# A second layer's attention weighed one sequence later, its chances transposed by VectorE and two trips through memory

## The chip, the cores and the metric

The kernel runs on one core of a Trainium2 chip. A core has five engines that work side by side, each with its own instruction queue: TensorE for matrix products (PE in the profile; PEld is its loading of weights), VectorE (DVE), ScalarE (ACT), GpSimd (POOL) and SyncE (SP), which here issues DMAs. Engines wait for each other by semaphores. The metric is the device time of one execution in microseconds (us), as the median of several runs.

## The reference, cut to what matters

The input is x, 8 sequences of 512 tokens with 256 channels, in f32. Two layers follow each other. The first (16 heads of attention with rotary embedding, plus a product with 8-bit weights) is not touched. The second, for each sequence b, is:

```python
xn = layernorm(x)
left, right = xn @ compare_left, xn @ compare_right            # 512 x 64 each
comparison = left @ right.T / sqrt(256)                        # 512 x 512
mask  = comparison > threshold
gated = softmax(comparison + gate_bias)
attn  = (mask * gated) @ xn
prev  = xn shifted by one token
xr, xk = mu_r * xn + (1 - mu_r) * prev, mu_k * xn + (1 - mu_k) * prev
ffn   = sigmoid(xr @ W_r.T) * (relu(xk @ W_k.T) ** 2 @ W_v.T)
out   = x + attn + ffn
```

`mask * gated` before its division by the row sums is called the chances below. The product `chances @ xn` needs the chances with keys in the partitions, while the comparison leaves them with queries in the partitions, so they are transposed in between.

## The kernel before

All of it is one program, written out instruction by instruction for each engine; nothing reorders it later. Each engine executes its instructions in the order in which the Python text issues them, so the order of the calls in the loop over sequences (`for b in range(B)`, L1002) is the order of work on every engine. Tiles come from pools whose buffers go round; a tile waits until the last reader of the buffer's former tile is done. PSUM has eight banks, handed out in turn by `bank`.

A sequence of layer 2 is made of these steps:

- `norm` (L223): mean and variance of x1 on DVE, the power -1/2 on POOL, and, in the function that it returns, four normalising operations on DVE.
- `turn_input` (L228): eight transposes on PE (`pyt`) and two copies by ACT give xn with channels in the partitions (`yt`).
- `sides_of` (L240): left and right by PE (`plr`), a copy by ACT, and two DMAs on SP's queue (L249, L250) that exchange the upper and lower halves of `lr`.
- `mix_before` and `mix_own` (L653, L662): the two mixtures with the token before, s = 1 for the key and s = 0 for the gate. ACT writes (1 - mu) times the token before, DVE adds mu times the token.
- `compare` (L670): four products `c`, their row maxima on DVE (L685, L689), the exponential with its row sums on ACT (L694), and on DVE the mask times the exponential (L697, tile `e`).
- `key`, `gate`, `value` (L703, L717, L731): the feed-forward part, products `pk`, `pg` and `pvv` on PE, the squares of kk and the sum with x1 on POOL, the product with the gate on DVE.
- `turn_chances` (L743): sixteen transposes on PE (`trc`, L749), and four copies out of PSUM, two by ACT and two by DVE, into `ptc`.
- `end` (L756): the weighing. 16 products `po` in two halves, whose weights are the transposed chances, the division by the row sums and the sum with the rest on DVE (L768), and the store of `y`.
- `clip_late`, `complete`, `round_late`, `fetch_late` (L644, L649, L641, L634): the last piece of layer 1 for sequences two and three ahead: a clip on DVE to bf16 (`xq`, L197 and L201), products `acc` on PE, `u` on DVE (L215), a sum on POOL (L218), and their loads.

In the loop, iteration b does compare and key of b, then the input, mixtures and sides of b + 1 in between the gate and value of b, then the transposes of b's chances, complete, and last the weighing of b itself, with the norm of b + 2 between its halves. Layer 1 uses a similar transposition for its own input: `turn_x` (L320) turns squares of 32 x 32 on DVE (L325) and moves them through memory.

Of the kernel before, what the change touches and what calls it, by code (L numbers as in the profile page):

```python
# [16 lines left out]
P = 128  # L17
B, S, D = 8, 512, 256
H, L = 16, 64
NT = S // P  # L20
# [24 lines left out]
def two_layers(  # L45
# [214 lines left out]
    with ExitStack() as c0:  # L260
# [151 lines left out]
        def finish(at):  # L412
            for half in range(2):
                output_product(at, half)
                add_output(at, half)
# [218 lines left out]
        def fetch_late(b):  # L634
            if b < B - 1:
                tag, k = {2: ("vr", 0), 3: ("vr", 1), 4: ("t1", 0), 5: ("t1", 1), 6: ("t2", 0)}[b]
                fetch_output(b, by_tokens(cuts[tag][k]))
            if b > 2:
                late[b] = fetch_input(b, cuts["wo"][b % 2])
# [4 lines left out]
        def clip_late(b):  # L644
            xq = work.tile([P, NK * S], BF16, tag="xq", name=f"xq_{b}")
            clip(late.pop(b), xq)
            return xq

        def complete(b, xq):  # L649
            for half in range(2):  # L650
                add_quantised(b, half, xq, line(f"u_{b}_{half}"))

        def mix_before(b, s):  # L653
            mx = work.tile([P, NK, S], F32, tag="yl"[s], name=f"mix_{b}_{s}", bufs=2)
            for k in range(NK):
                nc.scalar.activation(
                    mx[:, k, :], xts[b][:, k, :S], AF.Copy,
                    scale=nmus[:, s * NK + k : s * NK + k + 1],
                )
            mixed[b, s] = mx  # L660

        def mix_own(b, s):  # L662
            mx = mixed[b, s]
            for k in range(NK):
                nc.vector.scalar_tensor_tensor(
                    mx[:, k, :], xts[b][:, k, 1:], gs[:, s * NK + k : s * NK + k + 1], mx[:, k, :],
                    ALU.mult, ALU.add,
                )

        def compare(b):  # L670
            one, two = lr.pop(b)
            es = [qk.tile([P, 2, S], F32, tag="h0", name=f"e_{b}_{n}") for n in range(2)]
            nm = small.tile([P, NT], F32, tag="nm4", name=f"nm4_{b}", bufs=2)
            nb = small.tile([P, NT], F32, tag="nb4", name=f"nb4_{b}", bufs=2)
            sm = small.tile([P, NT], F32, tag="sm4", name=f"sm4_{b}", bufs=2)
            rs = small.tile([P, NT], F32, tag="rs4", name=f"rs4_{b}", bufs=2)
            cs_ = [bank(f"c_{b}_{i}") for i in range(NT)]
            for i in range(NT):
                left, right = (one, two) if i % 2 == 0 else (two, one)
                rows = slice(i % 2 * KC, i % 2 * KC + KC)  # L680
                nc.tensor.matmul(  # L681
                    cs_[i], left[rows, bass.ts(i, P)], right[rows, :], start=True, stop=True
                )
            for i, c in enumerate(cs_):
                nc.vector.tensor_reduce(nm[:, i : i + 1], c, AX.X, ALU.max, negate=True)  # L685
                if i % 2:

                    two_ = slice(i - 1, i + 1)
                    nc.vector.tensor_scalar(  # L689
                        nb[:, two_], nm[:, two_], tg[:, 1:2], tg[:, 1:2], ALU.subtract, ALU.add  # L690
                    )
            for i, c in enumerate(cs_):
                e = es[i // 2][:, i % 2, :]
                nc.scalar.activation(  # L694
                    e, c, AF.Exp, bias=nb[:, i : i + 1], accum_out=sm[:, i : i + 1]
                )
                nc.vector.scalar_tensor_tensor(  # L697
                    e, c, tg[:, 0:1], e, ALU.is_gt, ALU.mult
                )
            nc.vector.reciprocal(rs, sm)  # L700
            pcs[b], sums[b] = es, rs

        def key(b):  # L703
            xk = mixed.pop((b, 1))
            kk = prob.tile([P, NK, S], F32, tag="p", name=f"kk_{b}")
            for m in range(NK):
                pb = bank(f"pk_{b}_{m}")
                for k in range(NK):
                    nc.tensor.matmul(  # L709
                        pb, w2[:, 1, k, bass.ts(m, P)], xk[:, k, :],  # L710
                        start=(k == 0), stop=(k == NK - 1),
                    )
                nc.scalar.activation(kk[:, m, :], pb, AF.Relu)
                nc.gpsimd.tensor_tensor(kk[:, m, :], kk[:, m, :], kk[:, m, :], ALU.mult)
            return kk
# [15 lines left out]
        def value(b, half, r, kk):  # L731
# [8 lines left out]
            nc.vector.tensor_tensor(r[:, rows, :], pb, r[:, rows, :], ALU.mult)  # L740
            nc.gpsimd.tensor_tensor(r[:, rows, :], r[:, rows, :], x1s[b][:, rows, :], ALU.add)

        def turn_chances(b):  # L743
            es = pcs.pop(b)
            pt = [qk.tile([P, 2, NT, P], F32, tag="h1", name=f"ptc_{b}_{n}") for n in range(2)]
            for i in range(NT):
                tr = bank(f"trc_{b}_{i}").rearrange("p (m n) -> p m n", m=NT)
                for m in range(NT):
                    nc.tensor.transpose(tr[:, m, :], es[i // 2][:, i % 2, bass.ts(m, P)], ident)  # L749
                if i % 2 == 0:  # L750
                    nc.scalar.copy(pt[i // 2][:, i % 2], tr)
                else:
                    nc.vector.tensor_copy(pt[i // 2][:, i % 2], tr)
            return pt

        def end(b, ats, pt, r, y):  # L756
            rs, xn = sums[b], xns[b]
            for at in ats:
                po = bank(f"po_{b}_{at}").rearrange("p (j n) -> p j n", j=2)
                for j in range(2):  # L760
                    for m in range(NT):
                        nc.tensor.matmul(  # L762
                            po[:, j, :], pt[at // 2][:, j, m, :], xn[:, m, :],
                            start=(m == 0), stop=(m == NT - 1),
                        )
                for j in range(2):
                    i = at + j
                    nc.vector.scalar_tensor_tensor(  # L768
                        y[:, i, :], po[:, j, :], rs[:, i : i + 1], r[:, i, :],
                        ALU.mult, ALU.add,  # L770
                    )

                    if b == B - 1:
                        nc.sync.dma_start(out[b].rearrange("(t p) c -> p t c", p=P)[:, i, :], y[:, i, :])
                if b < B - 1:
                    nc.sync.dma_start(
                        out[b].rearrange("(t p) c -> p t c", p=P)[:, at : at + 2, :], y[:, at : at + 2, :]
                    )
# [220 lines left out]
            value(0, half, r, kk)  # L999
        compare(0)  # L1000
        finish(at)
        for b in range(B):  # L1002
            if b == 0:
                cut(prob, [P, 2, 4 * pitch(1) + 1, Q], "t1", 2)
                cut(prob, [P, 2, 4 * pitch(2) + 1, Q], "t2", 1)
                cut(work, [P, NP, D], "wo", 2)
            if b + 3 < B:
                fetch_late(b + 3)
            if b > 0:
                compare(b)  # L1010
                kk = key(b)
            if b + 1 < B:
                turn_input(b + 1, whole(f"yt_{b + 1}", S + 1))
            if b > 0 and b + 2 < B:
                xq = clip_late(b + 2)
            if b + 1 < B:
                mix_before(b + 1, 1)
                mix_own(b + 1, 1)
            if b == 0:
                pt = turn_chances(b)  # L1020
            else:
                r = gate(b)
            if b + 1 < B:
                sides_of(
                    b + 1, *(attp.tile([P, S], F32, tag="att", name=f"lr_{b + 1}_{n}") for n in range(2))
                )
            if b + 1 < B:
                mix_before(b + 1, 0)
            if b > 0:
                for half in range(2):  # L1030
                    value(b, half, r, kk)
            if b + 3 < B:
                round_late(b + 3)
            if b > 0:
                pt = turn_chances(b)
            if b + 2 < B:
                complete(b + 2, xq)
            if b + 1 < B:
                mix_own(b + 1, 0)
            y = work.tile([P, NT, D], F32, tag="v", name=f"y_{b}", bufs=2)  # L1040
            end(b, (0,), pt, r, y)
            if b + 2 < B:
                normal = norm(b + 2, by_tokens(cuts["t0"][(b + 2) % 3]))
            end(b, (2,), pt, r, y)
            if b + 2 < B:
                normal()


def _layouts(i):
# [63 lines left out]
```

## Time and profile before

| | before |
|---|---|
| median of 3 runs | 938.59 us (937.72 to 939.12) |
| the profiled execution | 939.52 us, span 937.7 us |
| granted TensorE clock | 0.996 |
| PE busy | 920.2 us, 98% |
| DVE busy | 794.8 us, 85% |
| ACT busy | 527.4 us, 56% |
| POOL busy | 543.3 us, 58% |
| one sequence of layer 2, 839.75 to 864.40 | 24.65 us: PE 24.65, DVE 21.00, ACT 12.59, POOL 10.09 busy |

The page's span counts from the first to the last instruction; the run's own time is 1.8 us longer. An engine's busy time says how much of the span it works, not whether it is waited for: that is read from the chain of waits, which follows each instruction back to what released it. Rows by tile give the shortest, median and longest duration in ns and the number of instructions. f32 products appear as two records each, so 16 products of `po` are 32 records.

### The profile page before, as it was taken

The page shows a single profiled execution, that of the slowest core. Times are in us where ns is not written, and L with a number is a line of the kernel's source. Part 1 is how long each engine was busy: PE and PEld are TensorE (multiplying, and loading weights), DVE is VectorE, ACT ScalarE, POOL GpSimd, SP SyncE. Part 2 cuts the span into 40 slices and gives each one's busy share as a digit, 9 for nine tenths or more (in the row PEclk, how much of TensorE's full clock was granted, in tenths as well). Part 3 has the DMA queues.
Part 4 walks back from the last instruction along what each step waited for, and adds up shares of the span by engine and source line. Part 5 has one row for each costly group of instructions (what it writes and reads, how often), then busy time and mean ns, then how long its engine had stood idle before and what let it go on. Part 6 is the DMA issues. An engine that isn't in the chain of part 4 may idle for free.

```text
span 937.7 us, 27410 instructions
## 1 busy us (share of the span) xinstructions
PE 920.2 (98%) x10443; PEld 595.8 (64%) x10443; DVE 794.8 (85%) x2443; ACT 527.4 (56%) x1476; POOL 543.3 (58%) x688
## 2 busy tenths in 40 slices
PE   8999998999999999999999999999999999999998
PEld 5446565666565666657575656566657777777776
DVE  4997789897989889988998899899899588888854
ACT  3575555555564656564657465556667434445553
POOL 2576667566665566476756756688666424444311
PEclk9999999999999999999999999999999999999999
DMA  6757454435552554346534645554444132221011
GB/s 205 200 154 195 110 128 148 111 88 135 171 121 77 134 168 112 101 99 182 136 74 120 177 108 123 172 143 107 101 116 126 48 101 75 71 59 45 23 34 34
DMA packets 68706, 108.55 MB, mean 116 GB/s; under 512 B 8416, under 2 KB 47328, under 8 KB 68576
## 3 DMA queue, kind: packets, MB, share of 16 engines
q1 hardware_dynamic: 66704, 105.16, 42.1%
q10 hardware_dynamic: 1872, 1.64, 0.7%
q8 instruction: 83, 1.36, 0.6%
q14 instruction: 47, 0.39, 0.1%
HBM read 42.29 MB, written 28.84 MB: 76 GB/s over the span
## 4 chain that ended last, share of the span: by engine, by line
PE 84%; DVE 7%; DMA 3%; issue 2%; POOL 2%; ACT 1%; SPq 1%; DVEq 0%; POOLq 0%; ACTq 0%
PE pq L434 20%; PE av L603 14%; PE sc L515 11%; PE pw L396 10%; PE pv L478 8%; PE po L762 6%; PE pk L709 3%; PE pg L724 3%; PE pvv L736 3%; DVE t L586 2%; DVE p L543 2%; PE c L681 2%; PE trc L749 1%; PE plr L245 1%; DMA y<-l 1%
## 5 line engine op out<-in xcount | busy, mean ns | idle before, releaser
L547 ACT ACTIVATE p<-p,nm 128x64 f32<-128x64 f32 (+15 forms) x512 | 260.0, 512 | 131.4 <-DVE nm L543 106.7
L566 POOL TENSOR_SCALAR p<-p,rs 128x512 f32<-128x512 f32 (+4 forms) x504 | 266.4, 552 | 44.6 <-DVE rs L558 42.5
L467 POOL TENSOR_TENSOR h<-h,y 128x1024 f32<-128x1024 f32 x62 | 161.2, 2599 | 184.3 <-DVE y L452 100.7
L543 DVE CUSTOM_DVE_ANT_0 p<-sc,cmask 128x64 f32<-128x64 f32 (+15 forms) x512 | 190.1, 434 | 52.2 <-PE sc L515 52.2
L586 DVE STREAM_TRANSPOSE t<-p 128x256 f32<-128x256 f32 (+3 forms) x640 | 192.1, 365 | 18.2 <-POOL p L566 18.2
L515 PE MATMUL sc<-h,h 64*32 64x512 f32 (+15 forms) x4096 | 137.7, 393 | 1.2 <-POOL h L467 1.2
L603 PE MATMUL av<-t,vr 32*64 32x256 f32 (+15 forms) x4096 | 130.3, 396 | 5.5 <-issue 5.5
L603 PEld LDWEIGHTS av<-t,vr 32*64 32x64 f32 x4096 | 124.3, 132 | 10.9 <-issue 9.6
L515 PEld LDWEIGHTS sc<-h,h 64*32 64x32 f32 x4096 | 78.2, 106 | 78.3 <-issue 57.7
L440 ACT ACTIVATE l<-pq,cs 128x512 f32<-128x512 f32 x128 | 84.6, 684 | 65.4 <-PE pq L434 54.3
L434 PE MATMUL pq<-xnT,wk 128*128 128x512 f32 x256 | 114.8, 601 | 3.6 <-DMA xnT<-xnf 2.4
L452 DVE TENSOR_TENSOR y<-y,cs 128x1024 f32<-128x1024 f32 x64 | 110.9, 1733 | 7.3 <-DMA y<-l 7.3
L396 PE MATMUL pw<-wo,att 128*128 128x256 f32 x512 | 114.9, 382 | 0.5 <-DVE nm L543 0.5
L434 PE MATMUL pq<-xnT,wq 128*128 128x512 f32 x256 | 114.6, 599 | 0.9 <-ACT xnT L352 0.9
L478 PE MATMUL pv<-wv,xnT 128*128 128x512 f32 x256 | 114.3, 599 | 0.0
L396 PEld LDWEIGHTS pw<-wo,att 128*128 128x128 f32 x512 | 95.9, 190 | 19.2 <-issue 6.1
L547 ACT ACTIVATION_READ_ACCUMULATOR p<-p,nm 128x1 f32 x512 | 97.5, 190 | 0.0
L434 PEld LDWEIGHTS pq<-xnT,wk 128*128 128x128 f32 x256 | 48.9, 192 | 61.5 <-issue 57.9
L452 DVE TENSOR_TENSOR h<-l,cs 128x1024 f32<-128x1024 f32 x64 | 80.0, 1251 | 4.9 <-ACT l L440 4.9
L478 PEld LDWEIGHTS pv<-wv,xnT 128*128 128x128 f32 x256 | 47.3, 190 | 57.9 <-issue 54.5
L434 PEld LDWEIGHTS pq<-xnT,wq 128*128 128x128 f32 x256 | 47.2, 190 | 56.6 <-issue 48.8
L617 ACT ACTIVATE att<-av,cs 128x512 f32<-128x512 f32 x64 | 38.8, 689 | 72.4 <-PE av L603 72.4
(114 smaller groups left out, 939.0 us busy)
## 6 DMA issues: line engine op xcount, KB each, us to landing
y<-l SPq DMA_DIRECT2D x256, 128.0 KB, 2.3
va<-v SPq DMA_DIRECT2D x32, 512.0 KB, 6.3
vr<-va SPq DMA_DIRECT2D x64, 256.0 KB, 5.0
x<-in_x SPq DMA_DIRECT2D x15, 512.0 KB, 4.2
x1f<-x SPq DMA_DIRECT2D x7, 512.0 KB, 4.3
out<-y SPq DMA_DIRECT2D x14, 256.0 KB, 2.2
xnf<-xs SPq DMA_DIRECT2D x6, 512.0 KB, 3.3
xnT<-xnf SPq DMA_DIRECT2D x24, 128.0 KB, 2.9
```

Source lines behind the costliest of these rows:

```text
L396: nc.tensor.matmul(pw[:, j, :], atts[at, p][:, tok], wo[:, 4 * (at % NH) + p, :], start=(p == 0), stop=(p == 3),)
L434: nc.tensor.matmul(pb.rearrange("p (t a r) -> p t a r", a=4, r=Q), w[:, g, k, bass.ts(t, P)], xnT[b][:, k].rearrange("p a (t r) -> p t a r ...
L440: nc.scalar.activation(l[:, t, :], pb, AF.Identity, bias=cs[:, bias : bias + 1])
L452: nc.vector.tensor_tensor(dst, src, table[:, None, :].to_broadcast([P, 2, S]), ALU.mult)
L467: (engine or nc.gpsimd).tensor_tensor(h, h, y, ALU.add)
L478: nc.tensor.matmul(pb.rearrange("p (g n) -> p g n", g=2), xnT[b][:, k, 2 * half + j], wqkv[2][:, 2 * g : 2 * g + 2, k, :], start=(k == 0), ...
L515: nc.tensor.matmul(scored[at, i][e][j * Q : j * Q + Q, :], q[rows, j % 2, bass.ts(i, Q)], k[rows, j % 2, :n], start=True, stop=True,)
L543: nc.vector.tensor_tensor_reduce(p[:, e, col : col + n], sc, cmask[:, S - n :], -1.0 / L**0.5, BIG, ALU.add, ALU.min, nm[:, c : c + 1],)
L547: nc.scalar.activation(p[:, e, col : col + n], p[:, e, col : col + n], AF.Exp, bias=nm[:, c : c + 1], scale=-1.0, accum_out=sm[:, c : c + 1],)
L566: nc.gpsimd.tensor_scalar(p, p, rs[:, c : c + 1], 1.0, ALU.mult, ALU.mult)
L586: nc.vector.transpose(turned[at][c][:, :, at_ : at_ + (n - 1) * pitch(c) + 1 : pitch(c), :], p[:, :, c * P : c * P + n * Q].rearrange("p e ...
L603: nc.tensor.matmul(banks[j][e * L : e * L + L, i * Q :], vs[at][rows, c, m, bass.ts(e, L)], t[c][rows, e, m * pitch(c) + m : m * pitch(c) ...
```

## The change

Four things change, all in layer 2.

1. For b = 1 to 6 the chances are no longer transposed on PE. In `compare`, after each pair of e operations, DVE transposes the 32 x 32 squares of the pair (two operations of 128 x 512), with the four column blocks written interleaved, so that the words of one block lie four words apart. Four DMAs on SP's queue store each of the two tiles to memory in pieces of 512 bytes. Later, four DMAs a tile load them back as rows of 4 KB, each square in its transposed place (`move`). `po` then takes its weights at every fourth word. b = 0 and b = 7 keep `turn_chances`.
2. The weighing of b = 1 to 6 (`end`) is done in iteration b + 1, after its comparison and key. The loads of b's own squares are issued behind it, and the norm of b + 1, which used to come with the weighing of b - 1, keeps its place between the halves of that weighing.
3. The order of the rest of an iteration: gate, `turn_input`, complete, `sides_of`, mixture 1, value, mixture 0. Before, mixture 1 of b + 1 stood ahead of the gate, and complete behind the value.
4. For b > 1, `mix_own` of s = 0 is done by ACT (a scaled copy into `own`) and POOL (a sum) in place of DVE.

```diff
         def mix_own(b, s):
             mx = mixed[b, s]
             for k in range(NK):
+                if b > 1 and s == 0:
+                    own = line(f"own_{b}_{k}")
+                    nc.scalar.activation(
+                        own, xts[b][:, k, 1:], AF.Copy, scale=gs[:, s * NK + k : s * NK + k + 1]
+                    )
+                    nc.gpsimd.tensor_tensor(mx[:, k, :], mx[:, k, :], own, ALU.add)
+                    continue
                 nc.vector.scalar_tensor_tensor(
...
+                if i % 2 and by_squares(b):
+                    moves.append(turn_squares(b, i // 2, es[i // 2]))
             nc.vector.reciprocal(rs, sm)
-            pcs[b], sums[b] = es, rs
+            pcs[b], sums[b] = moves or es, rs
...
+        def by_squares(b):
+            return 0 < b < B - 1
+
+        def turn_squares(b, n, e):
+            there = qk.tile([P, 4, 2, Q, NT], F32, tag="h1", name=f"stc_{b}_{n}")
+            for i in range(2):
+                nc.vector.transpose(
+                    there[:, :, i].rearrange("p m q c -> p c m q"),
+                    e[:, i, :].rearrange("p (c m k) -> p c m k", c=NT, m=4),
+                )
+            between = away.tile([Q, 4, 2, 4, Q * NT], F32, tag="sq", name=f"sq_{b}_{n}")
+            for a in range(4):
+                nc.sync.dma_start(
+                    between[:, :, :, a].rearrange("k m i x -> k (m i) x"),
+                    there[bass.ts(a, Q)].rearrange("k m i q c -> k (m i) (q c)"),
+                )
+            def move():
+                here = qk.tile([P, 2, 4, Q * NT], F32, tag="h1", name=f"ptc_{b}_{n}")
+                for m in range(4):
+                    nc.sync.dma_start(
+                        here[bass.ts(m, Q)].rearrange("k i a x -> k (i a x)"),
+                        between[:, m].rearrange("k i a x -> k (i a x)"),
+                    )
+                return here.rearrange("p i a (q c) -> p i c (a q)", c=NT)
+            return move
...
+        held = {}
         for b in range(B):
...
             if b > 0:
                 compare(b)
                 kk = key(b)
+            if b > 1:
+                end(b - 1, (0,), *held[b - 1])
+                if b + 1 < B:
+                    normal = norm(b + 1, by_tokens(cuts["t0"][(b + 1) % 3]))
+                end(b - 1, (2,), *held.pop(b - 1))
+            if by_squares(b):
+                pt = [move() for move in pcs.pop(b)]
+            if b > 1 and b + 1 < B:
+                normal()
+            if b > 0 and b + 2 < B:
+                xq = clip_late(b + 2)
+            if b > 0:
+                r = gate(b)
             if b + 1 < B:
                 turn_input(b + 1, whole(f"yt_{b + 1}", S + 1))
...
-            if b > 0:
+            if b == 0 or b == B - 1:
                 pt = turn_chances(b)
             if b + 2 < B:
                 complete(b + 2, xq)
             if b + 1 < B:
+                sides_of(
+                    b + 1, *(attp.tile([P, S], F32, tag="att", name=f"lr_{b + 1}_{n}") for n in range(2))
+                )
+                mix_before(b + 1, 1)
+                mix_own(b + 1, 1)
+            if b > 0:
+                for half in range(2):
+                    value(b, half, r, kk)
+            if b + 1 < B:
+                mix_before(b + 1, 0)
+            if b + 3 < B:
+                round_late(b + 3)
+            if b + 1 < B:
                 mix_own(b + 1, 0)
+            if by_squares(b):
+                held[b] = pt, r, y
+            else:
+                end(b, (0,), pt, r, y)
+                if b == 0:
+                    normal = norm(b + 2, by_tokens(cuts["t0"][(b + 2) % 3]))
+                end(b, (2,), pt, r, y)
+                if b == 0:
+                    normal()
```

More of the change, by code (lines that the diff above doesn't have):

```diff
@@ L691, in compare @@
                     )
+            moves = []
             for i, c in enumerate(cs_):
@@ L762, in end @@
                         nc.tensor.matmul(
-                            po[:, j, :], pt[at // 2][:, j, m, :], xn[:, m, :],
+                            po[:, j, :], pt[at // 2][:, j, m], xn[:, m, :],
                             start=(m == 0), stop=(m == NT - 1),
@@ L1008, in two_layers @@
                 fetch_late(b + 3)
+            y = work.tile([P, NT, D], F32, tag="v", name=f"y_{b}", bufs=2)
             if b > 0:
@@ L1011, in two_layers @@
                 kk = key(b)
+            if b > 1:
[11 more added lines that the diff above has]
+                r = gate(b)
             if b + 1 < B:
                 turn_input(b + 1, whole(f"yt_{b + 1}", S + 1))
[L1014 to L1019, printed above, removed]
+            if b == 0 or b == B - 1:
                 pt = turn_chances(b)
-            else:
-                r = gate(b)
+            if b + 2 < B:
+                complete(b + 2, xq)
             if b + 1 < B:
@@ L1026, in two_layers @@
                 )
-            if b + 1 < B:
-                mix_before(b + 1, 0)
+                mix_before(b + 1, 1)
+                mix_own(b + 1, 1)
             if b > 0:
@@ L1031, in two_layers @@
                     value(b, half, r, kk)
+            if b + 1 < B:
+                mix_before(b + 1, 0)
             if b + 3 < B:
                 round_late(b + 3)
-            if b > 0:
-                pt = turn_chances(b)
-            if b + 2 < B:
-                complete(b + 2, xq)
             if b + 1 < B:
                 mix_own(b + 1, 0)
[L1040 to L1046, printed above, removed]
+            if by_squares(b):
[7 more added lines that the diff above has]
+                    normal()
 def _layouts(i):
```

## The prediction

> **What bounds the kernel now.** I read the page's first part, then the chain of waits through layer 2, then the busy time of one sequence, then the rows of what the change touches. The edit lies wholly in layer 2's loop, from 765 us on, so its price is read there. The page's busy times, and one sequence of the loop (the row's columns: length, then busy time with instructions of PE, PEld, DVE, ACT and POOL, granted clock, DMA share, GB/s):
>
> ```profile
> PE 920.2 (98%) x10443; PEld 595.8 (64%) x10443; DVE 794.8 (85%) x2443; ACT 527.4 (56%) x1476; POOL 543.3 (58%) x688
> ...
> 839.75:864.40 24.65, 24.65 (x119) 18.39 (x118) 21.00 (x43) 12.59 (x23) 10.09 (x8) 1.00 0.19 54
> ```
>
> PE is never idle in those 24.65 us, at full clock, and DVE has 21.0 us of work. The chain in order of time over the same sequence (start, length, work):
>
> ```profile
> 839.75 1.92 PE c L681 x8
> 841.67 3.63 PE pk L709 x8
> 845.30 0.87 PE pyt L234 x8
> 846.18 3.52 PE pg L724 x16
> 849.70 1.72 PE plr L245 x4
> 851.41 3.45 PE pvv L736 x16
> 854.87 1.75 PE trc L749 x16
> 856.61 0.87 PE acc L209 x8
> 857.49 6.91 PE po L762 x32
> ```
>
> Only PE stands there: what leaves PE shortens the layer, as long as nothing makes PE wait. The rows that price the change (ns min/median/max, first and last start):
>
> ```profile
> L749 PEld LDWEIGHTS trc<-ident,e x128: 139/141/142, 754.4 to 926.6; 128*128 128x128 f32 x128
> L762 PEld LDWEIGHTS po<-cut_t,ptc x224: 190/190/192, 783.4 to 933.3; 128*128 128x128 f32 x112
> L325 DVE STREAM_TRANSPOSE xs<-x x12: 668/676/702, 151.4 to 599.6; 128x512 f32<-128x512 f32 x12
> L201 DVE TENSOR_SCALAR xq<-xq x8: 426/1144/1147, 598.5 to 873.6; 128x1024 bf16<-128x1024 bf16 x8
> L665 DVE SCALAR_TENSOR_TENSOR mix<-yt,gs,mix x32: 736/752/1754, 707.8 to 907.2; 128x512 f32<-128x512 f32 x32
> L249 SPq DMA_DIRECT2D lr<-lr x7: 467/467/468, 758.8 to 902.1; - x7
> ```
>
> Of the DMA issues, with KB and median us to landing:
>
> ```profile
> cut_wo<-xnf SPq DMA_DIRECT2D x12, 128.0 KB, 4.8
> ```
>
> L325 is the same transpose of squares in layer 1, with runs of 32 written together. L201 takes 0.43 us alone and 1.14 beside a POOL operation, L665 0.74 alone and up to 1.75.
>
> **Step 1, PE's transposes go.** Six sequences lose trc: 6 x 1.75 = -10.5 us, all on the path. ACT loses two copies of 0.59 each time, DVE two of 0.69.
>
> **Step 2, DVE's load.** Per squared sequence DVE gains four transposes. By L325 one is 0.676, and 0.6 where the next one overlaps it by 0.08, as e's four of 0.74 do in 2.72: +2.4 us. It loses the two copies (1.4) and, from b + 1 = 2 on, the two mix_0 operations, which beside POOL's L218 took 2.9 us together. So DVE has about 19 of 21 us left, PE 24.65 - 1.75 = 22.9. No row writes every fourth word as these do; bounds: 0.676 (nothing makes it faster than runs) and twice that, 1.35. I take 0.676, as it is the same operation, size and type.
>
> **Step 3, the new order, walked through one steady sequence** (us from the first c). PE: c to 1.92, pk to 5.55, po of the sequence before to 12.46, pg to 15.96, pyt to 16.83, acc to 17.70, plr to 19.42, pvv to 22.87. DVE: free of the last gate product at 0.9; four maxima with nb take 3.03 in the row (842.15 to 845.18), to 3.9; four e of 2.72 together and four transposes, to 9.1; first y to 10.0 (its po ended at 9.0); norm statistics 1.9, to 11.9; POOL's power 1.2, to 13.1; four normalisations 1.3, to 14.4; clip. In the old order clip took 2.14 because POOL squared kk beside it; now POOL is done at about 8.3, so the alone price holds (0.64 + 0.43): 15.5. PE needs the normalised input at 15.96 (1.5 to spare) and xq at 16.83 (1.3 to spare). This is the tightest place on DVE. The new waits before it queue the maxima, e, transposes, y, norm and clip on DVE; who waits behind them is pyt and acc on PE.
> ACT: sigmoid, yt copies, then lr's copy at 19.42 to 20.05; mix_before to 21.4, mix_own on DVE to 22.2, gate products to 23.7, where the next DVE period began. complete now stands ahead: its u takes DVE to 19.0 and POOL's two sums from 18.2 to 20.8, before mix_own's 20.8; if they meet, mix_own takes 2.9 (the row beside L218) for 1.4, and the 1.3 of slack is just used up. round_late (1.12 on POOL) goes ahead of the new adds. ACT's four extra passes for mix_0 (two of them new, 0.75 each) end near 1.2 of the next sequence, before nb at 2.3, with the 1.28 table load ending at 2.4: cover 0, cost if it goes 0.2. POOL's two adds (1.27 each by L218's lowest) end near 6.3 and pg reads them at 12.5; kk follows at 8.3 and pvv reads it at 19.4. Both are covered.
>
> **Step 4, DMAs.** Each squared sequence adds 16 issues of 128 KB on SP's queue: 8 stores in 512-byte pieces, 8 loads in 4 KB rows; the two out stores move between them. An issue is 0.3 to 0.6 us in the rows, 0.43 typical. Stores of the second half go out at 9.1 and are issued by 11; the second out store waits for y at 13.4; then 8 loads, issued by 17.2, landed by about 19.5 at 2.2 to 2.8 each. The next use of these tiles is po at 5.55 of the next sequence, 9 us later: hidden. lr's two swaps stand behind them on SP and are due at 20.05: SP is free 2.8 us before. lr lands 2.2 after its issue (rows), at 22.3 for the first, and c is due at 22.87: 0.5 to spare. Landing of the squares is bounded by 2.2 (lr, out) below and 6.3 (va, 512 KB) above; I take 2.5, as out also stores to memory in short rows and took 2.2.
>
> **Step 5, weights of po.** They are read at every fourth word. No row has it. Bounds: 0, and twice 0.190 a load, which would replace the 0.216 spacing: 32 x 0.164 = 5.2 us a sequence. I take 0: trc's loads of 0.141 each went at 0.109 spacing (16 in 1.75), so loads overlap each other, and po has 0.216 for one.
>
> **Step 6, the ends.** b = 1 has no po of an earlier sequence to cover its transposes. PE reaches acc at 9.9; DVE starts its maxima 2.1 after c (768.13 in the trace) and has 3.0 + 5.2 + 1.2 before xq is there, at 11.6: a wait of 1.7. Then lr's swap stands on SP behind loads that wait for the stores' landing (last transpose 10.3, stores issued by 12.1, landed 14.5, loads issued by 16.2): lr lands at 18.5, c was due at 17.7: 0.8. If DVE starts 1.1 later, as it would with a busier POOL, both grow, to 4.3 together. I take 3.4, between 2.5 and 4.3. b = 6 has no acc between pyt and plr: plr waits for ACT's copies of yt behind the sigmoid, 0.5.
> Sum: -10.5 + 3.4 + 0.5 = -6.6 us. The profiled execution took 939.52 (span 937.7 and 1.8 around it), 0.9 above the median 938.59; the difference is put on the median: 932.0.
>
> [...]
>
> **Rivals.**
> 1. DVE becomes the bound, as spread writes take 1.2 to 1.35 us. Against: L325. For: no row has the step. Of 4 x 0.67 = 2.7 us more, 1.4 is taken by the slack of step 3: 1.3 in each of four steady sequences, 2.5 in b = 1, 0.7 in b = 6, so at 1.35 us -6.6 + 8.4 = +1.8, 940.4; at 1.2 us some 936.8. Chance 0.18.
> 2. Slower: spread weight loads set po's pace. Place: 192 loads in six sequences; price: 0.164 each at most, +31.5 - 6.6, 963; at 0.30 a load 192 x 0.084 = +16, 948. It decides from 6.6 / 192 = 0.034 us over 0.216, a load of 0.25. Against it the overlap in trc; for it nothing but the unseen step. Chance 0.13.
> 3. The squares land late and lr's swap waits for them on SP in every sequence. For: 5.8 us was seen for cut_wo and 6.3 for va. Place: before c; from a landing of about 5 us on, each further us costs one in each of five sequences: at 6.3, 6.5 us, so no change, 938.5. Against: DMA share is 0.19 to 0.28 now. Chance 0.09.
> The forecast has 0.60.
>
> **How the numbers follow.** A measurement of this kernel tells about 0.2%, 1.9 us, from no change: faster means below 936.7. The forecast's own range is 930 to 934.5. Faster: 0.60 and a little under half of rival 1, 0.66; same: the rest of rival 1 near 937 and half of rival 3, 0.12; slower 0.22. The range goes from 929.5 (b = 1 without a wait for lr) to 942 (rival 1's and part of rival 3's upper end); beyond it lie rival 2 and the worst of 3, under 0.2.
>
> **What would show it.** Right: PE steady at 22.9 us a sequence, no PE idle but in b = 1 before acc and c, transposes near 0.68, po still 6.91 for 32. Wrong: transposes at 1.2 or more and PE waiting for xq (step 2); po over 7 us (step 5); c waiting for lr after b = 1 (step 4); DVE not free of the gate product by 0.9 (step 3).

## The result, and the profile after

| | before | after |
|---|---|---|
| median | 938.53 us (937.72 to 939.12, 4 runs) | 943.91 us (942.83 to 945.79, 4 runs) |
| ratio | | 1.0050, 95% interval 1.0028 to 1.0071 |
| the profiled execution | 939.52 us | 945.79 us |
| layer 2, from the first c to the end of the last product | 189.15 us | 194.95 us |
| a steady sequence | 24.65 us | 24.94 us |

The change made the kernel slower by 5.4 us by the medians (4.7 by the ratio) where 6.6 us less were forecast, and the time lies outside the range. The last two rows come from the starts of the products c in the traces. The part of a run that lies outside layer 2 executes the same instructions in all kernels here and took between 746.3 and 750.8 us in the profiled executions, so parts are compared below by the length of layer 2, and whole kernels by the ratio to before and its interval, as the tables give them (a ratio is not exactly the quotient of the two medians; the two differ by up to 0.1%).

The page's busy times of the kernel after:

```profile
PE 919.8 (97%) x10347; PEld 596.9 (63%) x10347; DVE 796.0 (84%) x2443; ACT 529.2 (56%) x1476; POOL 552.3 (59%) x700
```

PE is busy for hardly less time than before, and DVE, which was to lose work, has as much. Two stretches of layer 2, a steady sequence (b = 4) and that of b = 1, with the columns of the windows in the prediction:

```profile
838.20:863.14 24.94, 24.52 (x102) 18.64 (x101) 21.40 (x43) 12.98 (x24) 11.61 (x11) 1.00 0.52 137
766.40:789.22 22.82, 17.84 (x70) 11.29 (x69) 17.61 (x38) 11.81 (x23) 6.76 (x6) 0.93 0.70 179
```

In the steady one DVE is busy for 21.40 us where the forecast had 19, and PE is no longer busy all the time. At b = 1 PE is idle for 5 of 22.8 us, and the granted clock is 0.93. The chain of waits through the steady sequence (start, length, work):

```profile
838.20 1.07 PE c L688 x3
...
839.29 1.30 DVE nm L692 x2
...
840.62 1.19 DVE nb L696
841.81 1.19 DVE nm L692 x2
...
844.18 1.40 DVE e L705 x2
845.57 0.27 DVE stc L762
...
846.46 1.12 DVE stc L762
847.58 1.18 DVE e L705 x2
...
850.70 0.73 DVE y L810 x2
851.42 1.31 DVE st_b L153 x4
...
854.42 1.38 DVE cut_t L172 x4
855.80 0.61 DVE xq L197
...
856.43 0.43 DVE xq L201
...
856.92 1.05 PE acc L209 x8
```

Before, PE alone stood in this chain. Now it runs from c through DVE's work, with one POOL operation of 1.03 us in between (the power), to the clip (xq), for which `acc` waits: the wait that the prediction gave 1.3 us of slack. acc begins 18.8 us after the first c; undisturbed, by the blocks of this kernel (c 2.13, pk 3.54, po 7.45, pg 3.45, pyt 0.87), it would begin after 17.4. Two DVE links are out of proportion: nb, and the transposes `stc`. Their rows by tile, with that of the row maxima `nm`, and the weight loads of po (ns min/median/max):

```profile
L762 DVE STREAM_TRANSPOSE stc<-e x24: 1043/1114/1170, 773.9 to 898.7; 128x512 f32<-128x512 f32 x24
```

```profile
L692 DVE TENSOR_REDUCE nm<-c x32: 674/681/693, 746.4 to 915.6; 128x1 f32<-128x512 f32 x32
L696 DVE TENSOR_SCALAR nb<-nm,gs x16: 287/1042/1312, 747.7 to 916.3; 128x2 f32<-128x2 f32 x16
```

```profile
L804 PEld LDWEIGHTS po<-cut_t,ptc x224: 190/329/332, 794.9 to 939.6; 128*128 128x128 f32 x112
...
L804 PEld LDWEIGHTS po<-yn,ptc x32: 188/190/190, 759.0 to 765.9; 128*128 128x128 f32 x32
```

DVE's second nb in the steady sequence, and what POOL does beside the two nb (start, length):

```profile
843.02 1.24 DVE L696 TENSOR_SCALAR nb<-nm,gs 128x2 f32<-128x2 f32 x1
```

```profile
840.65 1.13 POOL L192 TENSOR_SCALAR cut_wo<-cut_wo,xs 128x1024 f32<-128x1024 f32 x1
841.74 2.50 POOL L670 TENSOR_TENSOR mix<-mix,own 128x512 f32<-128x512 f32 x2
```

A transpose with spread writes takes 1.11 us, not 0.676. nb, two columns wide, takes 0.29 us alone (b = 0 and 1) and up to 1.31 later. Reading every fourth word makes a weight load 0.329 us in place of 0.190 (the row with `yn` is b = 0, whose weights are contiguous). The chain at b = 1:

```profile
773.94 2.04 DVE stc L762 x2
...
778.01 1.04 DVE stc L762
...
779.64 0.43 DVE xq L201
...
780.12 1.85 PE acc L209 x8
781.97 2.61 PE plr L245 x4
...
785.62 3.46 DMA lr<-lr
...
789.22 2.65 PE c L688 x8
```

Here PE waits twice, as a view of all PE's waits in layer 2 sums up (total, number, longest):

```profile
PE acc L209 <- DVE yt L230: 4.7, 4, 3.8
PE c L688 <- DMA lr<-lr: 1.2, 1, 1.2
```

The DVE instruction named there is a small clearing right behind the clip, and the clip is what acc reads. After the 3.8 us of idle time, acc takes 1.65 us up to the next block in place of 0.87 and plr 2.63 in place of 1.72: the trace's clock record has half speed from 780.20 on, for 3.41 us. SP's queue over the same stretch, with the number of issues:

```profile
776.01 5.60 SPq L769 DMA_DIRECT2D sq<-stc  x8
781.78 3.73 SPq L777 DMA_DIRECT2D ptc<-sq  x8
785.62 0.52 SPq L249 DMA_DIRECT2D lr<-lr  x1
```

SP has no pause of over 0.2 us here: the swap of lr goes out when the loads of the squares have been issued, 0.4 us after ACT's copy of lr ended (785.19).

The sum over layer 2, from the lengths of PE's blocks, each to the start of the next:

| part | forecast | measured |
|---|---|---|
| trc, six times | -10.5 | -10.5 |
| po, 7.45 in place of 6.91, six times | 0 | +3.2 |
| b = 1: 22.83 in place of 24.58 - 1.75 - 7.00 = 15.83 | +3.4 | +7.0 |
| wait for xq and the normalised input, b = 3 to 5 | 0 | +3.3 |
| c, whose second operand lands late (b = 2 to 7) | 0 | +2.3 |
| b = 6, plr behind ACT's yt | +0.5 | +0.5 |
| sum | -6.6 | +5.8 |

### The profile page after: what moved, and what is told of

Read it like the earlier page. It is cut to its first block, busy times and chain, and to the rows that moved or that the text cites. A ratio compares the mean times of both kernels' runs of the same rounds, so it can differ in the third digit from the quotient of the medians.

```text
span 944.0 us, 27372 instructions
## 1 busy us (share of the span) xinstructions
PE 919.8 (97%) x10347; PEld 596.9 (63%) x10347; DVE 796.0 (84%) x2443; ACT 529.2 (56%) x1476; POOL 552.3 (59%) x700
## 4 chain that ended last, share of the span: by engine, by line
PE 75%; DVE 13%; DMA 4%; issue 3%; POOL 2%; ACT 2%; SPq 1%; DVEq 0%; POOLq 0%; ACTq 0%
PE pq L434 20%; PE av L603 14%; PE sc L515 11%; PE pw L396 9%; PE pv L478 7%; PE po L804 3%; DVE t L586 3%; PE pvv L746 3%; DVE p L543 2%; DMA y<-l 2%; PE plr L245 2%; PE pk L719 2%; PE pg L734 1%; PE c L688 1%; POOL p L566 1%
## 5 line engine op out<-in xcount | busy, mean ns | idle before, releaser
L603 PE MATMUL av<-t,vr 32*64 32x96 f32 (+15 forms) x4096 | 130.7, 396 | 4.5 <-issue 4.5
```

Source lines behind the costliest of these rows:

```text
L603: nc.tensor.matmul(banks[j][e * L : e * L + L, i * Q :], vs[at][rows, c, m, bass.ts(e, L)], t[c][rows, e, m * pitch(c) + m : m * pitch(c) ...
```

## The experiments

The theory from the trace: M1, spread writes lengthen DVE's transposes (0.43 us each, 1.7 a sequence); M2, nb is held by a POOL operation that now lies beside it (1.85 a sequence), and M1 and M2 together use up the 1.3 us of slack; M3, spread weights cost PE 0.54 a sequence; M4, the first sequence with squares has no weighing to lie over them. Each run was timed beside the kernel before on the same chip: its median was 937.38 us beside x1 to x4, 936.82 beside x5 to x8 and 937.86 beside x9 to x11.

| run | median us | ratio to before (95%) | layer 2, us | steady sequence, us |
|---|---|---|---|---|
| after | 943.91 | 1.0050 (1.0028 to 1.0071) | 194.95 | 24.94 |
| x1 without nb | 940.99 | 1.0033 (1.0020 to 1.0046) | 190.68 | 23.59 |
| x2 runs of 32 | 938.83 | 1.0018 (1.0002 to 1.0034) | 189.70 | 23.62 |
| x3 runs and weights | 937.40 | 1.0001 (0.9985 to 1.0017) | 189.19 | 23.61 |
| x4 b = 1 on PE | 943.08 | 1.0057 (1.0042 to 1.0073) | 196.52 | 24.87 |
| x5 b = 0 held | 940.06 | 1.0038 (1.0023 to 1.0053) | 191.54 | 24.94 |
| x6 without part 4 | 946.98 | 1.0111 (1.0093 to 1.0128) | 197.14 | 25.37 |
| x7 order only | 940.42 | 1.0040 (1.0025 to 1.0055) | 192.81 | 24.76 |
| x8 POOL later | 939.43 | 1.0019 (1.0006 to 1.0032) | 190.06 | 23.58 |
| x9 x5 and x8 | 935.11 | 0.9972 (0.9960 to 0.9984) | 186.99 | 23.59 |
| x10 x9, weights contiguous | 933.32 | 0.9957 (0.9940 to 0.9973) | 183.55 | 23.07 |
| x11 x10, runs of 32 | 931.46 | 0.9935 (0.9919 to 0.9951) | 182.78 | 23.03 |

### x1: nb left out

```diff
...
-                if i % 2:
-                    two_ = slice(i - 1, i + 1)
-                    nc.vector.tensor_scalar(
-                        nb[:, two_], nm[:, two_], tg[:, 1:2], tg[:, 1:2], ALU.subtract, ALU.add
-                    )
...
-                    e, c, AF.Exp, bias=nb[:, i : i + 1], accum_out=sm[:, i : i + 1]
+                    e, c, AF.Exp, bias=nm[:, i : i + 1], accum_out=sm[:, i : i + 1]
```

> The changed kernel without nb, the two small DVE operations that take the row maxima to the bias of the exponential and back; the exponential takes nm itself. What is left out is the rounding of that step alone. Theory A (nb, which stands beside a POOL operation since the change and ends with it at 1.0 to 1.3 us in place of 0.29, is a needed part of the stall): DVE gets back up to 1.8 us in each steady sequence, PE's wait for the normalised input and xq of about 1.5 us goes, so the steady period falls from 24.9 to about 23.4 and the whole by 5 to 6 us, to about 938; b = 1 keeps its waits. Rival B (the transposes of squares alone, 0.43 us over the forecast each, make the stall): a few tenths a sequence, 942 or more, and the steady period stays above 24.5. Rival C (the POOL operation holds whatever DVE does beside it): the row maxima lengthen instead by about as much, and the time stays near 943.

The steady sequence (b = 4) in the windows of x1:

```profile
835.37:858.96 23.59, 23.59 (x101) 18.69 (x100) 19.02 (x41) 12.86 (x24) 11.60 (x10) 1.00 0.55 144
```

PE is busy in all of it again, and DVE does 2.4 us less: twice 1.2. That is theory A; the maxima did not lengthen, so rival C is out, and rival B as well. Layer 2 fell by 4.3 us against 5 to 6 expected: b = 3 kept a c of 2.97 us. The median, 940.99 us, stayed above the 938 expected.

### x2: the transposes written in runs of 32

```diff
                 nc.vector.transpose(
-                    there[:, :, i].rearrange("p m q c -> p c m q"),
+                    there.rearrange("p m i q c -> p m i (q c)")[:, :, i].rearrange("p m (c q) -> p c m q", c=NT),
```

> The changed kernel, with the transposes of squares written in runs of 32 words in place of every fourth word; the words of a chance row then stand in another order than the weighing reads, so keys and queries are mixed up within a block: the values are not the reference's, the work is the same. Theory A (spread writes are the other needed part of the stall): the transposes fall from 1.11 to about 0.68 us, DVE gets back 1.7 us a sequence, the steady period falls from 24.9 to about 23.4 and the whole by 5 to 8 us (b = 1 gains up to 1.7 as well), to 936 to 939; po keeps its 7.45 us. Rival B (nb beside POOL alone makes the stall): the period stays above 24.5, the whole falls by at most the 1.7 of b = 1, 942 or more. If the spread does not set the transposes' time, they stay at 1.1 and nothing moves.

The row of the transposes in x2:

```profile
L762 DVE STREAM_TRANSPOSE stc<-e x24: 660/680/699, 770.7 to 889.3; 128x512 f32<-128x512 f32 x24
```

0.680 is what L325 of layer 1 had promised, so the spread of the writes alone makes the difference of 0.43 us. The steady sequence fell to 23.62 here as well. So neither M1 nor M2 is the cause alone: each alone fits into the slack, and together they pass it by about as much as either of them takes. Rival B is out.

### x3: contiguous weights too

```diff
-                return here.rearrange("p i a (q c) -> p i c (a q)", c=NT)
+                return here
```

(with the edit of x2)

> As the one with runs of 32, and the weights of po read as contiguous runs of 128 as well; the order of keys and queries within a block is mixed up, so the values are not the reference's, and the work is the same. Theory: weight loads fall from 0.33 to 0.19 us and the spacing of the products from 0.233 to 0.216, so po takes 6.91 in place of 7.45 us, and where PE is the bound that is 0.54 us in each of six sequences: 3.2 us below the run with the runs alone, about 933 to 936. Rival (spread weights are hidden, and the spacing came from something else in that part): the same time as the run with the runs alone, within 0.5 us.

po took 6.91 us, but the steady sequence stayed at 23.61: `pyt` took 1.44 to the next block in place of x2's 0.89, and gave the 0.54 back. DVE's chain, with nb still held, set the pace. Layer 2 fell by 0.5 us below x2 and the median by 1.4, where 3.2 were expected: c of b = 2 also ran at half clock (from 786.26 on, for 3.41 us) and took 3.96 us in place of x2's 2.41. The price of M3 had to be asked again where PE was the bound (x10).

### x4: b = 1 on PE

```diff
         def by_squares(b):
-            return 0 < b < B - 1
+            return 1 < b < B - 1
...
-            if b > 1:
+            if by_squares(b - 1):
                 end(b - 1, (0,), *held[b - 1])
...
```

(with the other conditions on b that follow from it)

> The changed kernel, with the chances of b = 1 transposed by PE and weighed in their own iteration, as before; b = 2 to 6 stay as in the change. Theory: b = 1 has no weighing to lie over its squares, so its waits (3.8 us of idle PE before acc, 1.7 us by the half clock after it, 1.2 us before c) go, and trc's 1.75 us come back, po loses 0.54: about 5 us less than the change, 938 to 939.5, and the granted clock shows no half-speed stretch near 780 us. Rival (whichever sequence is the first with squares pays, since it has no held weighing): the same idle time stands at b = 2, the whole within 1.5 us of 943.9. Rival 2 (the half clock is the throttle's own and comes with or without the idle time): the idle time goes, the half clock stays, 940 to 941.

The chain of x4 at b = 2, now the first with squares:

```profile
800.75 1.05 PE acc L209 x8
...
806.42 3.27 DMA lr<-lr
...
809.83 4.37 PE c L688 x8
```

The first rival was right: b = 1 is as before (24.57 us), and b = 2 has the waits, 2.9 us before acc and 2.9 before c, with half clock from 809.38 on for 6.8 us. It is not b = 1 that is special, but the first sequence with squares.

### x5: b = 0 held as well

```diff
-            if b > 1:
+            if b > 0:
                 end(b - 1, (0,), *held[b - 1])
...
                 sides_of(
                     b + 1, *(attp.tile([P, S], F32, tag="att", name=f"lr_{b + 1}_{n}") for n in range(2))
                 )
+                if b == 0:
+                    pt = turn_chances(b)
...
-            if by_squares(b):
+            if b < B - 1:
                 held[b] = pt, r, y
...
```

> The changed kernel, in which b = 0 is also weighed in the next iteration, behind the comparison and key of b = 1 (its chances still come from PE, behind the sides of b = 1; the norm of b = 2 moves with it). What x4 showed, that whichever sequence is the first with squares waits, is then to go. Theory (the first squared sequence waits because no held weighing of 7.0 us lies over its squares): PE's idle time before acc and c at b = 1 goes, with the half clock, and its period falls from 22.83 (without po) to about 23.7 with po; in exchange c of b = 1 waits for lr behind trc, about 2 us, in the period before. Together about 4 us less than the change, 939 to 940.5. Rival (the wait for lr is as long as what it replaces, 4 to 6 us, and brings the half clock): 942 to 945.

PE's waits in layer 2 of x5:

```profile
PE acc L209 <- DVE yt L230: 1.5, 5, 0.3
PE c L688 <- DMA lr<-lr: 1.2, 1, 1.2
```

The idle time of 3.8 us is gone, with it the half clock, and the exchange of lr costs one wait of 1.2 us, less than the 2 expected. Layer 2 fell by 3.4 us. M4 is shown: 7.0 us of products over the first squares are what was missing.

### x6: without part 4

```diff
-                if b > 1 and s == 0:
+                if b > B and s == 0:
                     own = line(f"own_{b}_{k}")
```

> The changed kernel without part 4: mixture 0 is DVE's again in every sequence, ACT and POOL do nothing for it. Theory A (nb ends with the POOL operation beside it): the second nb of a sequence, which stood beside POOL's add for mixture 0, falls from 1.24 to about 0.3; the first still stands beside the rounding and stays at about 1.2. DVE gives back 1.45 for the two mixture operations that it gets between the gate product and the maxima: the steady period grows by about 0.5, to 25.4, the whole is 944 to 947. Rival B (POOL's adds alone hold DVE up, the rest of nb's length is DVE's own): both nb fall to 0.3 and the whole falls by 2 or more, below 942.

The steady period of 25.37 us is the one expected, but for other reasons. Both nb fell to 0.29 us, since the maxima start so late that the rounding is over too. And the two mixture operations, as this line of the chain shows, took 2.74 us in place of 1.45, beside POOL's sums of the gate:

```profile
862.63 2.74 DVE mix L672 x2
```

So part 4 helped the change, by 2.2 us of layer 2. Theory A holds for nb, but POOL also slowed the two mixture operations beside it, and taking its work away from one place only moved the loss. x6 shows one thing more at b = 1: PE waited 3.8 us for acc as in the kernel after, but the clock stayed full, and b = 1 still took 22.50 us against 22.83, because PE then waited 2.6 us for lr in place of 1.2.

### x7: the order alone

```diff
-                if i % 2 and by_squares(b):
-                    moves.append(turn_squares(b, i // 2, es[i // 2]))
...
-                pt = [move() for move in pcs.pop(b)]
+                pt = turn_chances(b)
```

> Parts 2 to 4 alone: the later weighing, the order and mixture 0 as in the change, but the chances of every sequence transposed by PE and copied out of PSUM, behind the held weighing, where the change issues the loads of its squares. Theory: PE does the work of before in another order; per sequence 0.2 us more for c, which lost an overlap of its first products, and at b = 1 a wait of about 2.3 us for e, since trc stands right behind key there. About 3 to 4 us over before, so the order takes about half of what the change lost in it, 941 to 942.5. Rival (the order costs nothing where DVE has no squares to do): within 1 us of before, 937 to 939.5.

As expected: 3.6 us over before, of which 2.3 at b = 1 (19.89 us in place of 24.58 - 7.00 = 17.58). c takes 2.10 to the next block in place of 1.92 here too, so these 0.2 us come with the order and not with the squares. At b = 2 and 3, where the kernel after has a c of 2.58 and 2.69, x7 has 2.10 and 2.13: there the squares add 1.0 us, as the second swap takes 3.6 and 2.9 us to land in place of 2.3. The trace shows why: in the order before, the second swap of lr was issued at 853.33 for a c at 864.3, 11 us ahead; now (kernel after) it is issued at 860.88 for a c at 863.1, and PE's queue waits for it until 863.2.

### x8: POOL's work moved behind key

```diff
+        adds = []
+
+        def add_own():
+            for mx, own in adds:
+                nc.gpsimd.tensor_tensor(mx, mx, own, ALU.add)
+            adds.clear()
...
-                    nc.gpsimd.tensor_tensor(mx[:, k, :], mx[:, k, :], own, ALU.add)
+                    adds.append((mx[:, k, :], own))
...
                 kk = key(b)
+                add_own()
+                if b + 2 < B:
+                    round_late(b + 2)
...
-            if b + 3 < B:
-                round_late(b + 3)
```

> The changed kernel with POOL's rounding and its two adds for mixture 0 issued behind the squares of key in the next iteration, so that at the time of nb POOL has only the two sums of the gate (it does the same work as the change, and all of it). Theory A: the second nb falls from 1.24 to 0.3, the first to 0.3 to 0.7, the steady period from 24.9 to about 23.6, as without nb, and the whole to 939.5 to 941. Rival (the moved operations hold up what now stands beside them on DVE: y, the statistics, or the clip at the end of that stretch): nb falls, another DVE row grows by as much, and the whole stays at 943 or more.

nb and the steady sequence (b = 4) in x8:

```profile
L703 DVE TENSOR_SCALAR nb<-nm,gs x16: 286/288/290, 746.4 to 909.1; 128x2 f32<-128x2 f32 x16
```

```profile
834.66:858.24 23.58, 23.58 (x102) 18.68 (x101) 19.67 (x43) 12.87 (x24) 11.61 (x10) 1.00 0.54 144
```

All sixteen nb take 0.29 us, with the same work on POOL as after (11.61 us in that stretch), and the stall is gone. No other DVE row grew by as much; the transposes stand beside POOL's adds now and take 1.13. Theory A holds.

### x9: both edits together

The edits of x5 and of x8.

> The edits of x5 and x8 together: b = 0 is held and weighed in the next iteration as well, and POOL's rounding and adds stand behind the squares of key. Theory (the two waits are separate, so their gains add): from x5's first two periods of 15.52 and 24.14 and x8's others of 23.94, 23.93, 23.58, 23.58, 23.27 and 28.85, less 0.7 of x5's stall at b = 1, layer 2 takes 186.1 us against 189.15 before: 3 us less than before, a ratio of 0.996 to 0.998. Rival (with b = 0 held, POOL and DVE meet at b = 1 and 2 as at b = 1 of the change): the gain of one of the two is lost, within 1 us of before.

The ratio is 0.9972 (0.9960 to 0.9984): this version is faster than before and than after. Layer 2 took 186.99 us for 186.1 expected; c of b = 3 had 2.92 us, since the second swap of lr landed 0.9 us after c had begun, and b = 1 kept 0.7 of its stall.

### x10 and x11: the spread accesses taken out of x9

x10 has the edit of x3's diff on top of x9, x11 that of x2 as well. Both mix up keys and queries within a block, so they show what the spread accesses cost and are no kernels to use.

> x9 with the weights of po read as contiguous runs of 128: keys and queries are mixed up within a block, so the values are not the reference's, and the work is the same. Theory (spread weights cost PE 0.54 us in each of six sequences wherever PE is the bound, which it was not in x3): po 6.91 in place of 7.45, the steady period 23.04, 3.0 to 3.3 us below x9. Rival (DVE is still the bound or close to it): pyt or acc waits for as much, and the time is within 1 us of x9.

> x10 with the transposes written in runs of 32 as well, so both forms of spread access are gone; the values are not the reference's for the same reason. Theory (the slower transposes lie beside other work as soon as nb no longer waits): transposes 0.68 in place of 1.12, the steady period as in x10 within 0.1, the whole within 1 us of x10. Rival (the transposes set the pace of x10): the period falls by up to 0.5, the whole by 2 to 3 us.

The steady sequence in x10, and then in x11:

```profile
830.17:853.24 23.07, 23.07 (x102) 17.17 (x101) 19.52 (x43) 12.87 (x24) 11.62 (x10) 1.00 0.56 147
```

```profile
826.42:849.45 23.03, 23.03 (x101) 17.21 (x100) 18.34 (x43) 12.87 (x24) 11.61 (x10) 1.00 0.56 147
```

Where PE is the bound, spread weights cost 23.59 - 23.07 = 0.52 us a sequence, and layer 2 fell by 3.4: M3 is shown. Once nb is free, spread writes cost nothing in a steady sequence (23.07 against 23.03), though DVE works 1.2 us more; layer 2 fell by 0.8, nearly all at b = 1, where pyt went from 1.60 to 0.87. The medians fell by 1.8 and 1.9 us; with intervals of 1.5 us to either side they agree with both expectations but would not have decided them, and the lengths within the traces do.

## Why the prediction was wrong

**Step 1** held: trc left PE's path, and its 10.5 us are in the sum.

**Step 2** failed. "I take 0.676, as it is the same operation, size and type": the price was 1.11, in the upper half of the bounds, and x2 shows that only the writes' spacing makes it. The bounds, the author's estimate from the row, were right; the row was chosen over the one thing in which the two operations differ. Rival 1 had the mechanism, but not the size of the loss: 1.11 us alone, as x8 shows, fits into the slack.

**Step 3** failed in one term. The clip came out as worked out (0.69 and 0.43 us, without a POOL operation beside it), and DVE was free of the gate product 0.8 us after c. But "four maxima with nb take 3.03 in the row" was read in a place where POOL was idle. The new order puts POOL's gate sums, rounding and adds there, and nb takes 1.19 and 1.24 us. The step called those POOL operations covered because nobody waits for their results early; it did not ask which DVE operation they run beside, though it did for the clip and the mixture. DVE was ready for acc at 18.7 us in place of 15.5: nb brought 1.85 of it and the transposes 1.7, and 0.3 came back elsewhere. Against 1.3 of slack, widened to some 1.9 because PE came later too (po +0.54, c +0.2), 1.35 us of waiting were left.

**Step 4** held for the squares: sq landed in 2.4 us and ptc in 3.4 (medians) and no weighing waited for them, although an issue of a store took 0.61 us and not 0.43. For lr it gave the first swap 0.5 us to spare and left out the second, which came 0.1 to 0.7 us after the first c in every sequence: +2.3 us. That is what remains of rival 3.

**Step 5** failed in size: 0 was taken, 0.54 us a sequence was measured, far below the upper bound of 5.2. Loads of 0.329 us do overlap, as the step argued, but not entirely: the spacing of po's products went from 0.216 to 0.233 us. Rival 2 put the turning point at a load of 0.25, as if nothing overlapped; loads of 0.33 cost 3.2 us, and not the 22 of that reckoning (192 x 0.113).

**Step 6** had the mechanism at b = 1 and the wrong sizes: 7.0 us in place of 3.4, above its 4.3. The wait for acc was 3.8 and not 1.7; with the transposes in runs of 32 (x2) it is 2.5. What ends the stretch is the swap of lr behind the squares on SP: it was issued 19.2 us after c and not 16.2, as the last transpose ended at 12.7 and not 10.3 and the issues took longer, and it landed after 3.5 us and not 2.2. The half clock (acc 0.78 and plr 0.91 over their usual blocks) was in no term, but it mostly lay over that wait: in x3 and x6, where acc and plr of b = 1 ran at full clock, PE waited 2.6 us for lr, and b = 1 took 21.28 us (21.31 in x2, with the half clock) and 22.50 us (22.83 after). The bound of 4.3 does not follow from the step's own walk either: a DVE that starts 1.1 us later delays c as well as lr, so only the first wait grows, to 3.6 together. b = 6 was right.

With all of that taken out, x11 is 6.4 us faster than before by its median, and its steady sequence takes 23.03 us for the 22.87 walked through in step 3. The walk's order of work on PE and DVE holds; the prices put into it, and the place of POOL's work, did not. The fastest version here that computes the reference's layer is x9, 2.8 us below before.

**Not settled.** Why a spread write costs DVE 0.43 us is not shown beyond the spacing. The 0.2 us of c were traced to the second swap, but no run moved the swaps.

## What to carry to other kernels

When a change moves work on one engine, list for each stretch what now runs beside it on DVE and POOL, small operations too: a 0.29 us operation became 1.24, and moving three POOL operations by 5 to 8 us won the time back without removing any work. Two causes that each fit into the slack can exceed it together, so price them together; taking away either one then looks like the whole cure. Work put off by one iteration leaves the first one uncovered: ask what lies over it there.

## What the runs showed of the hardware

**POOL beside DVE: nb was held, the maxima were not.** nb ended about 0.03 us after the POOL operation beside it (in the steady sequence nb at 840.62 to 841.81, the rounding at 840.65 to 841.78; nb at 843.02 to 844.26, the add at 842.96 to 844.24). The maxima between them kept their 0.681, though POOL's first add ran beside them (841.74 to 842.96). With those POOL operations moved away (x8) all sixteen nb took 0.29. No run shows why the one operation was held and the other was not.

**Half clock after idle time, in six gaps of ten.** In after, PE was idle for 3.8 us before acc at b = 1, and the clock fell to 0.5 for 3.41 us. In x2 half clock followed idle time of 2.5 us. In x6 3.8 us before acc and 2.6 before c were not followed by it: its clock record has no half speed up to the end of layer 2. The granted clock of its window at b = 1, beside that of x2:

```profile
764.66:787.15 22.49, 16.16 (x69) 10.54 (x69) 19.35 (x40) 11.54 (x21) 8.13 (x7) 1.00 0.69 181
```

```profile
763.20:784.51 21.31, 17.67 (x70) 11.25 (x69) 16.30 (x38) 11.78 (x23) 6.73 (x6) 0.92 0.72 190
```

In x5, x7 and x9 to x11, whose longest idle time in layer 2 was 1.3 us, the clock stayed full up to the end of layer 2. Of the ten gaps of 2.5 to 3.8 us on PE in layer 2 of these runs, six were followed by half clock (after, x1, x2, x8 and the second gap of x3 and of x4) and four were not (the first of x3 and of x4, both of x6). What a half clock cost depended on what followed: 1.5 us on c of b = 2 in x3, where PE was the bound, and 0.0 to 0.3 at b = 1, where PE would have waited for lr anyway.
